# A quantised convolution and an involution on one core: each image's weights two stages earlier

## The chip, the cores and the metric

The kernel runs on one core of one Trainium2 chip. The metric is the device time of one execution in microseconds (us). The time before is the median of three runs, 1355.05 us (1355.0 to 1357.66). One further execution was profiled, and every row quoted from a profile is from it.

## What is computed

The input is a batch of 32 images with 256 channels of 32 x 32 pixels. Two layers follow each other, and each adds its result to its own input:

```
x = x + conv3x3_quantised(groupnorm(x)) + bias
x = x + involution(groupnorm(x))

involution(x):                       # 16 groups of 16 channels, 7 x 7 window
    y = relu(bn(w1 @ x))             # 256 -> 64 channels, per pixel
    w = w2 @ y + b2                  # 16 groups x 49 taps, per pixel
    out[g, c, pixel] = sum over 49 taps of w[g, tap, pixel] * x[g, c, neighbour(tap)]
```

The quantised convolution works on values rounded to ten mantissa bits, for which the kernel uses float16 operands. What is special about the involution is that its 7 x 7 weights differ from pixel to pixel: they must be computed for each image (784 of them per pixel) before the sums over neighbours can be made.

## The kernel before

**Engines and stages.** The program is written as one loop over stages (`for n in range(FRONT, B * per + 2)`, line 556), with `per = 16` stages to an image. Under `tc.manual_schedule()` each engine executes its instructions in the order in which the program issues them, so the order of the calls inside a stage is the order on every queue. `due(n, lag)` (line 549) turns a stage into an image `b` and a position `i` in 0..15: a step with lag -18 belongs to the image whose sums begin 18 stages later. Several images are therefore in work at once.

What an image `b` goes through, with stages counted from the start of its own sums (stage 0):

- Stage -63 (`LOAD`): its input `x` is loaded by SP, two DMAs (line 106). The tile pool has five image buffers, so this load waits for the output of image `b - 5`.
- Stages -56 to -7 (`FRONT`, the generator `front`): first group norm on ACT (lines 214 to 273), the 3 x 3 convolution on TensorE (line 332, nine matmuls in each odd stage), its clamp and residual add on DVE (lines 346, 348), second group norm, and at stage -20 the features: eight matmuls `py` (line 377), then two ACT activations that write `y_sb[b % 2]` (line 388). After that the normalised pixels are transposed by TensorE (`pt`, line 396) and copied by ACT into `pixels` (line 400).
- Stages -18, -16, ..., -4 (`LEAD = 18`, `weights`): eight blocks of 32 small matmuls `pw` (line 411), each for four image rows, that multiply `w2` with `y`. DVE adds the bias and writes the result into `w_sb` (line 435), a ring of 32 rows, that is one image. An inner block has four such evictions; the first and the last block of an image have eight smaller ones, because the window leaves the image there.
- `scatter` (line 465): when the rows of a quarter `k` (eight image rows) are complete, SP writes them from `w_sb` to `wd`, a DRAM buffer that holds one image. A quarter has seven DMAs of 160 KB (line 476): the four even ones one stage after the block that completes the quarter (blocks 2, 4, 6 and 7), the three odd ones one stage later. With the lag of 18 the four quarters start at stages -13, -9, -5 and -3. A quarter's rows in `wd` may be overwritten only once the previous image's band load of this quarter has read them.
- `load_bands` (line 478) at stages -9, -5, -1 and 3: a quarter's weights come back from `wd` in a skewed order into one of three `band` buffers, 16 DMAs (line 497), two issued by SP (`BY_SYNC`) and fourteen by POOL. The first needs all seven writes of its quarter and the buffer free from the sums three quarters before.
- Stages 0, 2, ..., 14: `sums`, 64 matmuls on band and pixels (line 522), two stages' worth to a quarter; one stage later DVE adds the result into `x` (line 538).
- Stages 12 and 15: `store` sends the two halves of the result out by SP (line 543).

**The order inside a stage** is: the fronts of all images in work, oldest first; `sums`; `add_windows` and `store`; `weights`; `scatter`; `load_x`; `load_bands`. So on TensorE a stage with features has `py`, then 64 sums matmuls of the image two before, then a block of weights matmuls of whichever image is due. Before the change the block in the stage of image `b`'s features is the last block of image `b - 1`.

**Queues.** SP issues input loads, weight writes, two sixteenths of the bands and the outputs, in order. POOL issues nearly nothing but its band transfers. Each of the two queues has eight semaphores for its DMAs in turn, so a DMA also waits for the one eight before it on its own queue.

Of the kernel before, what the change touches and what calls it, by code (L numbers as in the profile page):

```python
# [71 lines left out]
LATE = K1 * SW + 2 * 2 * SW  # L72
FRONT = -56
LOAD = -63
LEAD = 18


@with_exitstack
def tile_quant_conv_then_involution(
# [460 lines left out]
    def store(b, k):  # L540

        cols = slice(k * NT, (k + 1) * NT)
        nc.sync.dma_start(out[b].rearrange("(h p) n -> p h n", p=P)[:, :, cols], x_tiles[b][:, :, cols])
# [5 lines left out]
    def due(n, lag):  # L549

        b, i = divmod(n - lag, per)
        return (b, i) if 0 <= b < B else (None, None)

    with tc.manual_schedule():
        fronts = {}
        for n in range(FRONT, B * per + 2):
# [24 lines left out]
            if b is not None and i == 2 * (M - 1 - SIDES):  # L581
                store(b, 0)
            b, i = due(n, -LEAD)
            if b is not None and i % 2 == 0:
                weights(b, i // 2 * WR)

            for part in range(2):
                b, i = due(n, -LEAD + 1 + part)
                if b is not None and i % 2 == 0:
# [48 lines left out]
```

## Time and profile before

| | |
|---|---|
| median of the runs | 1355.05 us (1355.0 to 1357.66) |
| the profiled execution | 1344.24 us |
| its span, from the first to the last instruction | 1342.5 us |
| mean granted TensorE clock | 0.982 |
| data moved by DMA | 361.85 MB, mean 270 GB/s |
| weight writes, `wd<-w_sb` | 896 DMAs of 160 KB |
| band transfers issued by POOL / by SP | 1792 / 256 |
| one POOL band transfer: issue / from issue to landing | 549 ns / 4.6 us median |
| DVE waiting for weights matmuls | 419.2 us |
| POOL waiting for its own earlier band transfers | 182.0 us |
| POOL waiting for weight writes | 63.2 us, 37.1 of them once, at the start |
| PE waiting for bands | 42.7 us |
| SP waiting for outputs before it may load the next input | 77.1 us |

The table's waits are from the view that lists who waited for whom. An engine's wait costs time only if the engine is on the path that sets the end. DVE waits a lot here since it has the least to do. In the lists of groups, a row reads: line, engine, operation, what is written and read, shapes, count, then busy time and mean duration of one in ns, then the idle time before such instructions and what ended it. In the table of stretches an engine's figure is its busy time in that stretch, followed by the number of instructions; the last three columns are the granted TensorE clock, the mean busy share of the 16 DMA engines by packet time (overlapping packets can take it a little over 1), and GB/s.

### The profile page before, as it was taken

How to read it: one execution, taken by the hardware profiler on the slowest of the kernel's cores; microseconds unless marked ns; L12 is line 12 of the kernel's file. 1: busy time of each engine (PE TensorE's matmuls, PEld its weight loads, DVE VectorE, ACT ScalarE, POOL GpSimd, SP SyncE). 2: the span in 40 equal slices, each digit the busy share in tenths (PEclk: the TensorE clock that was granted, in tenths of full speed). 3: DMA queues.
4: the chain of work that ended last, by engine and by line, in shares of the span. 5: the costliest groups of instructions: out<-in, count | busy, mean ns of one | idle time of the engine just before them, and what ended most of it. 6: DMA issues, size and time to landing. Idle time of an engine off the chain costs nothing.

```text
span 1342.5 us, 65799 instructions
## 1 busy us (share of the span) xinstructions
PE 1253.6 (93%) x27648; PEld 763.7 (57%) x27648; DVE 818.8 (61%) x2539; ACT 733.3 (55%) x1731; POOL 1014.4 (76%) x1818
## 2 busy tenths in 40 slices
PE   5899999999999999999999999999999999999665
PEld 2356566565555655556655556666555566556454
DVE  3466666565666665656665666766666666666442
ACT  5775656455656556556545655655556564553300
POOL 9067878777787778777778787788777877788785
PEclk9999999999999999999999999999999999999987
DMA  6089999999999999999999999999999999999995
GB/s 228 11 237 295 271 293 293 279 266 281 272 286 282 291 285 270 283 263 280 293 282 283 270 288 282 293 297 296 281 288 275 277 284 290 271 281 266 278 274 166
DMA packets 360724, 361.85 MB, mean 270 GB/s; under 512 B 75056, under 2 KB 304752, under 8 KB 359152
## 3 DMA queue, kind: packets, MB, share of 16 engines
q1 hardware_dynamic: 278512, 229.38, 56.8%
q0 software_dynamic: 81920, 128.28, 33.9%
q8 instruction: 220, 3.60, 1.1%
q14 instruction: 72, 0.59, 0.1%
HBM read 176.60 MB, written 180.76 MB: 266 GB/s over the span
## 4 chain that ended last, share of the span: by engine, by line
PE 60%; DMA 23%; POOL 7%; issue 3%; ACT 3%; DVE 2%; SPq 1%; POOLq 0%; DVEq 0%; ACTq 0%
PE pc L332 25%; PE acc L522 19%; DMA band<-wd 17%; PE pw L411 11%; POOL band L497 7%; DMA wd<-w_sb 6%; PE pt L396 3%; PE py L377 3%; ACT junk L214 1%; SPq L476 1%; DVE w_sb L435 1%; DMA x<-in_x 1%; ACT xn L273 0%; SPq L497 0%; ACT xq L273 0%
## 5 line engine op out<-in xcount | busy, mean ns | idle before, releaser
L497 POOL DMA_DIRECT2D band<-wd x1792 | 980.3, 549 | 315.7 <-DMA band<-wd 182.0
L435 DVE TENSOR_TENSOR w_sb<-pw,late_sb 128x224 f32<-128x224 f32 (+7 forms) x1280 | 330.4, 322 | 419.5 <-PE pw L411 419.2
L332 PE MATMUL pc<-xq,wq 128*128 128x496 f16 (+3 forms) x2304 | 535.2, 379 | 20.3 <-ACT xq L273 18.3
L522 PE MATMUL acc<-band,pixels 64*32 64x190 f32 (+1 forms) x16384 | 426.6, 332 | 51.8 <-DMA band<-wd 42.7
L522 PEld LDWEIGHTS acc<-band,pixels 64*32 64x32 f32 x16384 | 304.7, 107 | 159.7 <-issue 81.1
L332 PEld LDWEIGHTS <-wq 128*128 128x128 f16 x2304 | 206.7, 98 | 316.1 <-issue 102.7
L411 PE MATMUL pw<-late_sb,y 64*32 64x224 f32 (+1 forms) x8192 | 288.9, 333 | 10.8 <-issue 9.4
L538 DVE TENSOR_TENSOR x<-acc,x 128x380 f32<-128x380 f32 (+1 forms) x512 | 262.0, 512 | 32.2 <-PE acc L522 23.2
L411 PEld LDWEIGHTS pw<-late_sb,y 64*32 64x32 f32 x8192 | 186.5, 106 | 38.1 <-issue 21.0
L400 ACT COPY pixels<-pt 128x512 f32<-128x512 f32 x128 | 73.7, 576 | 228.6 <-PE pt L396 228.6
L214 ACT ACTIVATE junk<-x 128x512 f16<-128x512 f32 (+1 forms) x192 | 146.4, 763 | 14.7 <-DVE x L348 12.2
L214 ACT ACTIVATE junk<-x,mean 128x1024 f16<-128x1024 f32 x128 | 147.1, 1149 | 4.3
L245 ACT ACTIVATE s<-back,eps 128x2 f32<-128x2 f32 x64 | 18.9, 296 | 178.6 <-DVE back L230 178.6
L346 DVE TENSOR_SCALAR q<-pc 128x512 f16<-128x512 f32 x128 | 87.2, 681 | 17.6 <-PE pc L332 17.6
L273 ACT ACTIVATE xn<-x,off,rstd 128x512 f32<-128x512 f32 x128 | 96.2, 800 | 0.0
L348 DVE SCALAR_TENSOR_TENSOR x<-q,early_sb,x 128x512 f32<-128x512 f16 x128 | 94.2, 736 | 0.3
L396 PEld LDWEIGHTS pt<-ident,xn 128*128 128x128 f32 x512 | 63.9, 142 | 26.3 <-issue 2.5
L396 PE MATMUL pt<-ident,xn 128*128 128x128 f32 x512 | 78.0, 275 | 0.1
L273 ACT ACTIVATE xq<-x,off,rstd 128x1024 f16<-128x1024 f32 x64 | 75.7, 1227 | 0.0
L235 ACT ACTIVATE mean<-back 128x2 f32<-128x2 f32 x64 | 12.6, 196 | 101.4 <-DVE back L230 101.4
L377 PE MATMUL py<-xn,early_sb 128*64 128x512 f32 x256 | 62.2, 606 | 0.9 <-ACT xn L273 0.9
L224 DVE STREAM_TRANSPOSE across<-sums 128x32 f32<-128x32 f32 x128 | 26.3, 205 | 33.6 <-ACT junk L214 32.4
(40 smaller groups left out, 369.3 us busy)
## 6 DMA issues: line engine op xcount, KB each, us to landing
wd<-w_sb SPq DMA_DIRECT2D x896, 160.0 KB
band<-wd POOLq DMA_DIRECT2D x1664, 70.5 KB, 4.6
x<-in_x SPq DMA_DIRECT2D x64, 512.0 KB
out<-x SPq DMA_DIRECT2D x64, 512.0 KB
band<-wd POOLq DMA_DIRECT2D x128, 60.5 KB, 4.6
band<-wd SPq DMA_DIRECT2D x128, 50.5 KB
band<-wd SPq DMA_DIRECT2D x128, 40.5 KB
band<-in_w SPq DMA_DIRECT2D x2, 1152.0 KB
```

What stands on the lines that cost most here:

```text
L214: nc.scalar.activation(junk[:, n0:n1], src[:, h, n0:n1], func, bias=bias, accum_out=self.sums[:, i : i + 1])
L273: nc.scalar.activation(dst, src, AF.Identity, bias=self.off[:, one], scale=self.rstd[:, one])
L332: nc.tensor.matmul(pc.rearrange("p (r c) -> p r c", c=W)[:, r0 - nt * RT : r1 - nt * RT, c0:c1], wq[:, kh, k, mh * P : (mh + 1) * P], xq[: ...
L346: nc.vector.tensor_scalar(q, pc, F16_MAX, -F16_MAX, ALU.min, ALU.max)
L348: nc.vector.scalar_tensor_tensor(xt[:, mh, cols], q, bias_sb[:, mh : mh + 1], xt[:, mh, cols], ALU.add, ALU.add)
L377: nc.tensor.matmul(py[i * CR : (i + 1) * CR], w1_sb[:, kh, :], px[:, :, i], start=kh == 0, stop=kh == CH - 1,)
L396: nc.tensor.transpose(pt[:, i, h * P : (h + 1) * P], xn[:, h, (m + i) * P : (m + i + 1) * P], ident)
L411: nc.tensor.matmul(pws[i][t * TW : (t + 1) * TW, : dj.stop - dj.start, r], y_sb[b % 2][half, (r0 // 2 + r) * W : (r0 // 2 + r + 1) * W], w ...
L435: nc.vector.tensor_tensor(to, of[:, :, d0:d1], bias[:, :, d0:d1], ALU.add)
L497: queue.dma_start(to, src)
L522: nc.tensor.matmul(at[t * TW : (t + 1) * TW, h, :, f - top : l - top], px[p, a, v * GC : v * GC + TW], of[:, :, a, f - top : l - top, v], ...
L538: nc.vector.tensor_tensor(x_at, of, x_at, ALU.add)
```

## The change

One constant changes:

```
-LEAD = 18
+LEAD = 20
```

`LEAD` is used in three places: `weights` (line 583) and both parts of `scatter` (line 588). All eight blocks of weights matmuls of an image, the evictions that follow them and the 28 writes to `wd` are issued two stages earlier with respect to that image's features, sums and band loads. The numbers of instructions stay as they are.

- The blocks now stand at stages -20, -18, ..., -6. The first one is issued in the stage of the image's own features: on TensorE `py`, the sums of another image, then the weights matmuls that read the `y` which ACT computes from `py`.
- The writes of the four quarters start at stages -15, -11, -7 and -5; the band loads stay at -9, -5, -1 and 3. Between a quarter's last write in program order and its band load there are now five stages instead of three (seven instead of five in the fourth quarter).
- A quarter's writes stand ten stages (eight in the fourth quarter) behind the previous image's band load of that quarter, instead of twelve (ten).
- On SP's queue, the four even writes of a first quarter now stand ahead of the input load of a later image, and its three odd writes right behind it; all seven stood behind that load. The even writes of a fourth quarter now stand ahead of the two SP band pieces of the second quarter, and its odd writes behind the first output; the whole quarter stood after that output.

## The prediction

> **What bounds the kernel now.** I read the page's first, third and fifth parts, then stretches of equal length, then the waits of POOL over the steady middle, then the chain of waits around one load, and last the rows of single instructions. The sum is made against the profiled execution: span 1342.5 us, 1344.24 us with what lies around it, which is 10.8 us under the median of the runs, 1355.05 us. I work out a difference and apply it to the median.
>
> ```profile
> span 1342.5 us, 65799 instructions
> PE 1253.6 (93%) x27648; PEld 763.7 (57%) x27648; DVE 818.8 (61%) x2539; ACT 733.3 (55%) x1731; POOL 1014.4 (76%) x1818
> ...
> DMA  6089999999999999999999999999999999999995
> ...
> q1 hardware_dynamic: 278512, 229.38, 56.8%
> q0 software_dynamic: 81920, 128.28, 33.9%
> ...
> L497 POOL DMA_DIRECT2D band<-wd x1792 | 980.3, 549 | 315.7 <-DMA band<-wd 182.0
> ...
> L522 PE MATMUL acc<-band,pixels 64*32 64x190 f32 (+1 forms) x16384 | 426.6, 332 | 51.8 <-DMA band<-wd 42.7
> ```
>
> Three things are nearly full at once: PE (93%), the DMA engines (56.8% for SP's transfers and 33.9% for POOL's) and POOL. POOL's busy 76% understates it. In the rows of its 1,792 band transfers, 14 to a load, 128 loads, the next load nearly always starts where the last ended, from 71.7 us to 1330.6 us; in between stand 980 us of issuing and the rest waiting. PE in its turn waits 42.7 us for bands.
>
> ```profile
> core 0: us, PE busy (x) PEld busy (x) DVE busy (x) ACT busy (x) POOL busy (x), PEclk, DMA share, GB/s
> ...
> 881.00:919.00 38.00, 38.00 (x866) 23.27 (x865) 25.32 (x80) 22.83 (x55) 31.34 (x58) 1.00 0.98 293
> 919.00:957.00 38.00, 38.00 (x865) 23.15 (x863) 25.25 (x79) 22.67 (x54) 29.33 (x54) 1.00 0.98 289
> 564.00:605.00 41.00, 38.35 (x857) 23.52 (x840) 24.16 (x77) 21.91 (x53) 30.14 (x56) 0.96 0.93 265
> ```
>
> Each of these is one image. In the first two PE never stops: 38.0 us is its floor. The third takes 41 us. By the first sums of images 0 and 29 (87.7 and 1236.1 us) the mean is 39.6 us, so 1.6 us an image is what no PE work explains.
>
> ```profile
> POOL band L497 <- DMA band<-wd: 168.0, 213, 2.9
> POOL band L497 <- issue: 50.7, 66, 3.2
> POOL band L497 <- DMA wd<-w_sb: 22.5, 24, 3.1
> ```
>
> These are POOL's waits from 103.4 to 1220.6 us. Only the third line is a wait for the weights' writes, which the change moves. The first is POOL waiting for its own transfers of eight before.
>
> ```profile
> 632.41 1.26 DVE w_sb L435 x4
> 633.67 0.47 DVE x L538
> ...
> 635.21 4.00 DMA wd<-w_sb
> ...
> 639.24 0.55 POOL band L497
> 639.79 4.86 DMA band<-wd
> ```
>
> The chain runs from the eviction over a write to POOL, but this link is doubtful: the POOL transfer at 639.24 is the last of its load, whose writes had been issued by 624.9 and had let its first transfer go at 630.9. So the page's share of 6% for wd<-w_sb is too high a price, and I count waits by their place in the load.
>
> **The change, part by part.** Nothing is added or removed; the 32 blocks of `weights` matmuls, their evictions and the 28 writes per image on SP stand two stages (of 16 per image, so 39.6/8 = 4.95 us) earlier against features, sums and band loads.
>
> POOL, the gain. Loads 4 to 115 are 28 of each quarter. A first transfer waits for the writes 12.8 us in all at the first quarter, 0.4 at the second, 2.3 and 3.4 at the third and fourth. At three of the latter (1.6, 1.8, 1.6 us) the last write had been issued 14 us or more before, so I leave both quarters out and take 13.2 us. The earlier start covers it: the longest of these waits is 1.9 us against 4.95. At the first quarter not all of 4.95 arrives, because the three odd writes now stand behind the next x load, but the four even ones stand ahead of it; four issues at about 0.83 us (seven took 5.76 us) still leave 3.3 us. Bounds: 0 to all 22.5 us.
>
> What comes back. Issuing sooner raises the share that SP's transfers take while POOL issues. Inside a load POOL waits 0.84, 2.22, 1.79 and 2.80 us in the four quarters, while SP's transfers take 0.52, 0.62, 0.54 and 0.66 of the DMA engines: 11.9 us per unit of share by a line through the four. An image shorter by x raises the mean share, 0.58, by 0.58x/39.6, and four loads then wait 4 × 11.9 × 0.58/39.6 = 0.70x longer. So the gain is 13.2/1.70 = 7.8 us, and with 22.5 it would be 13.2; with no feedback at all 22.5, with a full one 0.
>
> Here a rule speaks against the change. The row: during POOL's waits for writes the DMA engines were 1.02 busy by packet time, over 90 to 1240 us 0.965. The Trainium skill, "DMA: Bandwidth & Descriptors", section "Issuing engines are not separate DMA queues", says that transfers started by SP and POOL run on the same 16 engines and interleave; then an earlier write only makes a band transfer wait in its stead. By the rule the sum is 0 and the time 1355; by the row's 3.5% of free time something is left.
>
> PE, the loss. An image's first weights now stand in the stage of its features, behind 64 sums matmuls only, and need both y activations. y ends 1.07 to 1.40 us after the last py matmul, and the block that stands there now starts 1.17 to 1.25 us after it; its start would be held until 0.05 us after y, as it was at image 0. Over images 2 to 31 that is 3.3 us. At images 0 and 1 no sums stand between and y ends 3.0 us after py: PE idles 3.1 us each instead of 1.05 and 0.16, 4.9 us more. Behind the waiting matmuls stands the next convolution, and no band load waits for that. All 8.2 us are costed at nothing because PE waits 42.7 us for bands anyway; without that cover they cost 8.2 us.
>
> DVE and ACT. The two edge blocks take 1.89 us of evictions instead of 1.52 and move from stages 12 and 14 to 10 and 12; the narrowest margin of the sums' banks is 2.55 us, so nothing. ACT's order around y is the same.
>
> SP. A fourth quarter's writes overwrite what the previous image's fourth band load reads. That load's end plus the median 4.6 us to landing lies on average 0.5 us behind the eviction two stages earlier, behind it in 17 of 27 images, at most by 2.9 us, 16.9 us in all. Behind it on SP stand the odd writes, two band pieces, the first output and, four stages on, an x load. SP's band pieces are issued well before POOL's end; x lands 3.3 to 10.6 us before its first use. So nothing again; with that cover gone, the longest would cost 2.9 us an image. In exchange the four even writes of a first quarter stand ahead of the x load, where SP waits 77.1 us for outputs (2.9 us an image).
>
> The start: image 0's features end at 52.6 us and its weights start 3.07 us later in either order, so the first load moves by nothing. The end: the last loads are POOL's pace too, and gain nothing of their own.
>
> Sum: −7.8 us, 1355 − 8 = 1347 us; by the bounds 1332 to 1355.
>
> **The rivals.** "PE sets the pace": with the writes out of the way and SP not idle behind the x load, POOL gets ahead and all images take PE's 38.0 us. 29 × 1.6 = 46 us, less 10.8 us that PE loses before its own weights matmuls and 8.2 us at y: −27, 1328 us. For it: four images in a row (805 to 957 us) ran so, and buffers were free some 9 us before POOL used them. Against: in those four POOL's lead over PE shrank from 8.9 to 5.1 us, so POOL was the slower there too.
>
> "Nothing, since the wait changes its name": POOL waits for its own transfers just as long; 1355 us. For it: 1.02 busy in these waits. Against: 0.965 over all.
>
> "The writes now meet the first quarter's loads" (slower): first-quarter loads are the quick ones because SP's share is low there (0.52). With the writes two stages earlier these loads meet the third and fourth quarters' writes without a pause. If their inner wait rises from 0.84 to the mean of the four, 1.91, that is 1.07 × 31 = 33 us, less the 13.2: +20, 1375 us; if half of it comes back from the other quarters, +3, 1358. I take the middle, 1366. It decides from 13.2/31 = 0.42 us more per first-quarter load. For it: POOL has no slack, and the bunching is real: the pause between fourth- and first-quarter writes, which x and an output fill now, keeps only the output. Against: SP's total is unchanged, so other loads should gain what these lose.
>
> **How the numbers follow.** Forecast 0.37, PE's pace 0.13, nothing 0.15, slower 0.35. A measurement of this kernel can't tell less than about 0.2% (2.7 us) from no change. Faster is the first two, 0.50; same 0.15; slower 0.35. The likeliest time is the forecast's 1347 us, its own range 1332 to 1355. The range for 8 in 10 must hold both signs: from 1330, which leaves out the larger half of "PE's pace", to 1370, which leaves out a third of "slower".
>
> **What would show it.** The wait of POOL for wd<-w_sb should fall from 22.5 us over the same loads to under 5, and POOL's wait for its own transfers rise by 3 to 8 us from 168. If the first falls and the second rises by as much, it is "nothing"; by over 15 us more, and most of it in first-quarter loads, "slower". If images of 38.0 us become the rule and PE's wait for bands before the last three images falls below 10 us, it is "PE's pace". PE's wait for y should be about 9 us, 6 of them before 100 us; if it is over 20, my price of y was wrong. SP should show a new wait of some 15 us of fourth-quarter writes for band<-wd. The prediction is wrong if the first-quarter loads still wait for their writes, or if x lands late and ACT waits for it.

## The result and the profile after

The change makes the kernel slower. Its median over 12 runs is 1366.83 us (1362.56 to 1371.55), that of the kernel before, over 12 runs in turn with it, 1355.03 us (1347.15 to 1362.26). The ratio is 1.009, with a 95% interval from 1.0064 to 1.0116; the medians differ by 11.8 us. The profiled execution of the changed kernel took 1371.3 us and that of the kernel before 1344.24 us. The first is among the longest of its 12, the second shorter than all 12, so some 15 of the 27 us between the two spans are chance. What follows is read from places in the traces, not from the difference of the spans.

From the page of the changed kernel, its busy times and its groups of instructions:

```profile
span 1369.5 us, 65800 instructions
...
PE 1259.5 (92%) x27648; PEld 759.3 (55%) x27648; DVE 819.5 (60%) x2539; ACT 733.8 (54%) x1731; POOL 1014.6 (74%) x1818
...
L497 POOL DMA_DIRECT2D band<-wd x1792 | 980.5, 549 | 341.6 <-DMA band<-wd 215.0
...
L522 PE MATMUL acc<-band,pixels 64*32 64x190 f32 (+1 forms) x16384 | 429.4, 331 | 52.5 <-DMA band<-wd 25.6
...
L411 PE MATMUL pw<-late_sb,y 64*32 64x224 f32 (+1 forms) x8192 | 288.5, 330 | 27.5 <-issue 21.3
```

The work is the same: POOL still issues for 980 us. Its waits rose from 315.7 to 341.6 us. PE stands idle before the sums for as long as before (52.5 us against 51.8), but a smaller part of that is for bands (25.6 against 42.7). Before the weights matmuls it now stands 27.5 us, where it stood 10.8.

POOL's waits in the same stretch as shown for the kernel before, 103.4 to 1220.6 us (in all, times, longest):

```profile
POOL band L497 <- DMA band<-wd: 195.2, 251, 3.0
POOL band L497 <- issue: 42.0, 65, 2.5
POOL band L497 <- DMA wd<-w_sb: 13.6, 21, 1.8
POOL band L497 <- DMA x<-in_x: 7.6, 8, 1.8
```

The wait for the writes fell from 22.5 to 13.6 us, as the change suggests. The wait for POOL's own transfers rose from 168.0 to 195.2 us, three times as much, and 7.6 us of waits are put down to the input load, after 0.6.

Two images of the changed kernel, and then PE's waits from 140 to 1220 us, first of the changed kernel, then of the kernel before:

```profile
core 0: us, PE busy (x) PEld busy (x) DVE busy (x) ACT busy (x) POOL busy (x), PEclk, DMA share, GB/s
698.70:737.00 38.30, 38.30 (x865) 23.24 (x864) 25.27 (x80) 22.28 (x55) 29.34 (x54) 1.00 0.98 285
817.50:859.20 41.70, 39.21 (x871) 23.52 (x875) 24.39 (x78) 21.78 (x54) 33.52 (x62) 1.00 0.95 272
```

```profile
PE pw L411 <- issue: 17.5, 18, 1.8
PE acc L522 <- issue: 12.1, 11, 2.3
PE acc L522 <- DMA wd<-w_sb: 7.7, 8, 1.9
...
PE acc L522 <- DMA band<-wd: 0.9, 1, 0.9
```

```profile
PE acc L522 <- DMA band<-wd: 15.3, 13, 2.7
PE pw L411 <- issue: 8.2, 13, 1.1
PE acc L522 <- issue: 3.6, 5, 1.2
```

Some images still run without a stop, others take over 41 us. From the first sums of image 1 to those of image 29 an image takes 40.16 us on average, against 39.66 before. PE waits less for late bands (about 9 us, the lines of `wd<-w_sb` and `band<-wd` together, against 15 to 18) and far longer for nothing that the profile names: 31 us by "issue" against 12. One such stop on PE's timeline, in the midst of the 64 matmuls of a sum:

```profile
1033.65 0.56 PE L522 MATMUL acc<-band,pixels 64*32 64x190 f32 x15
1036.22 1.37 PE L522 MATMUL acc<-band,pixels 64*32 64x190 f32 x49 [2.01 <-issue]
```

After 15 of 64 matmuls PE executes nothing for 2 us, and the profile names no wait. The profile has a DMA queue of its own for instructions, the page's "q8 instruction": 220 transfers of 16,384 bytes, about one for every 256 instructions of PE. Four of the stops and the transfer that ended before each, from the trace of the changed kernel, in us:

```
PE stops   PE goes on   instruction transfer, start to end   from its end to PE
 351.01      353.36          350.82 to 351.92                     1.44
 393.04      394.63          392.25 to 393.36                     1.27
 480.02      481.71          479.29 to 480.22                     1.49
 833.82      835.58          833.18 to 834.30                     1.28
```

From 140 to 1220 us, all 24 unnamed stops over 0.25 us of the changed kernel, and all 17 of the kernel before, ended 1.2 to 1.8 us after the end of such a transfer, though one comes only every 6 us or so. So I read them as PE waiting for its own instructions; no run tried this alone. They gather in the fourth sums of an image: 20.2 us there after the change, 8.4 before.

### The profile page after: what moved, and what is told of

The parts are those of the page before. It is cut to its first block, busy times and chain, and to the rows that moved or that the text cites. A ratio compares the mean times of both kernels' runs of the same rounds, so it can differ in the third digit from the quotient of the medians.

```text
span 1369.5 us, 65800 instructions
## 1 busy us (share of the span) xinstructions
PE 1259.5 (92%) x27648; PEld 759.3 (55%) x27648; DVE 819.5 (60%) x2539; ACT 733.8 (54%) x1731; POOL 1014.6 (74%) x1818
## 4 chain that ended last, share of the span: by engine, by line
PE 76%; DMA 10%; issue 4%; ACT 4%; POOL 3%; DVE 2%; SPq 1%; POOLq 0%; ACTq 0%
PE pc L332 31%; PE acc L522 24%; PE pw L411 14%; DMA wd<-w_sb 7%; PE py L377 4%; PE pt L396 3%; POOL band L497 3%; DMA band<-wd 3%; ACT junk L214 1%; DVE w_sb L435 1%; SPq L476 1%; DMA band<-in_w 1%; ACT xn L273 0%; ACT xq L273 0%; ACT rstd L266 0%
## 5 line engine op out<-in xcount | busy, mean ns | idle before, releaser
L497 POOL DMA_DIRECT2D band<-wd x1792 | 980.5, 549 | 341.6 <-DMA band<-wd 215.0
L522 PE MATMUL acc<-band,pixels 64*32 64x190 f32 (+1 forms) x16384 | 429.4, 331 | 52.5 <-DMA band<-wd 25.6
L522 PEld LDWEIGHTS acc<-band,pixels 64*32 64x32 f32 x16384 | 301.4, 107 | 166.7 <-issue 93.5
L411 PE MATMUL pw<-late_sb,y 64*32 64x224 f32 (+1 forms) x8192 | 288.5, 330 | 27.5 <-issue 21.3
L538 DVE TENSOR_TENSOR x<-acc,x 128x380 f32<-128x380 f32 (+1 forms) x512 | 262.6, 513 | 39.5 <-PE acc L522 30.7
L224 DVE STREAM_TRANSPOSE across<-sums 128x32 f32<-128x32 f32 x128 | 26.3, 206 | 30.5 <-ACT junk L214 29.4
```

Source lines behind the costliest of these rows:

```text
L411: nc.tensor.matmul(pws[i][t * TW : (t + 1) * TW, : dj.stop - dj.start, r], y_sb[b % 2][half, (r0 // 2 + r) * W : (r0 // 2 + r + 1) * W], w ...
L497: queue.dma_start(to, src)
L522: nc.tensor.matmul(at[t * TW : (t + 1) * TW, h, :, f - top : l - top], px[p, a, v * GC : v * GC + TW], of[:, :, a, f - top : l - top, v], ...
L538: nc.vector.tensor_tensor(x_at, of, x_at, ALU.add)
```

## The experiments

Each is compared with the kernel before, run beside it on the same chip, whose median was 1355.31 us for e1 to e4, 1348.26 for e5 to e8, 1345.22 for e9 to e12, 1346.23 for e13 to e16 and 1345.41 for e17 and e18. "POOL" below is the time from the start of POOL's load 4 to the end of its load 115 in the one profile of each: 1108.8 us before, 1126.4 us after the change. "Stops" are PE's stops from 140 to 1220 us, the unnamed ones (by my reading, for instructions) + the others, mostly for late bands: 12.4 + 17.8 before, 31.3 + 9.2 after. Both are from one execution, and executions of one kernel differ by about 1% (1347.15 to 1362.26 us before the change), so the ratios decide and not these two.

**Is it the start, or the features' `y`?** Three edits of the changed kernel: the features one stage earlier (e1), image 3's input ahead of image 0's first writes (e2), and both (e3).

```
e1, e3:  in front(), before py:   stages(2) -> stages(1)
         in front(), after y:     stages(5) -> stages(6)
e2, e3:  ahead of the scatter loop:
+            if due(n, LOAD) == (3, 0):
+                x_tiles[3] = load_x(3)
```

> The kernel after, with the features (py and the two y activations) one stage earlier, so that a convolution half stands between py and the first weights again. Theory START (the +12 us are paid once, before the first sums: PE idles 3.1 us twice for y, runs at half clock after each, and reaches image 0's first sums 8.1 us later in the profiles): PE's wait for y falls from 6.2 to about 1 us, no half clock before the first sums, first sums at about 88 us instead of 95.8 if the bands are there; POOL's first load still starts at 76.6, so part stays: 1360 to 1363. Theory STEADY (the writes now collide with the band loads and SP's order is worse, some 0.4 us in each image): 1365 to 1368.

> The kernel after, with image 3's input load issued ahead of image 0's first writes, where it stood before the change, instead of between the even and the odd ones. START: POOL's first load starts at about 72 us instead of 76.6, since 1 MB no longer stands among the first writes; PE is late by y all the same, so 1362 to 1366. STEADY: no change, 1365 to 1368.

> The kernel after, with both: features one stage earlier, image 3's load ahead of the first writes. START: the first sums and the first load are where they were before, and the time is that of before or a little under it, 1348 to 1357. STEADY: 1364 to 1368. In between by the share of each.

Measured: e1 1364.9 us, 1.0064 [1.0037, 1.0091]; e2 1367.21 us, 1.0091 [1.0057, 1.0124]; e3 1362.39 us, 1.0061 [1.0032, 1.009]. In e2 POOL's first load starts at 71.0 us, where it started before the change (71.7, after it 76.6), and yet POOL takes 1126.3 us: the start is not the cause. `y` is at most a small part of it: e1's interval overlaps the change's.

**The weights early, the writes where they were.**

```
+WRITE = 18
-                b, i = due(n, -LEAD + 1 + part)
+                b, i = due(n, -WRITE + 1 + part)
```

> Weights and evictions two stages earlier as in the change, but the writes to DRAM left at their old stages. START by y alone: PE is late as in the change, POOL's first load starts near 72 us: 1360 to 1364. STEADY: the writes are where they were, so 1354 to 1358. If it is slower than the change, the early writes were a help and the early weights the harm.

Measured: 1354.56 us, 0.9993 [0.9966, 1.0019]; POOL 1109.8 us, stops 15.5 + 9.5. The whole loss goes with the writes. PE's order is that of the change, its first sums start at 96.4 us instead of 87.7, and nothing is lost by it: PE's waits for late bands fall by 8.3 us, about what the start is late.

**Which writes, and past what.** e5 writes only the first quarter early, e6 only the other three. e7 is the whole change with the input load moved ahead of the writes of its stage, so that all seven stand behind it again; e8 is the change with the input load two stages later, behind all seven.

```
e5, e6:  b, i = due(n, 1 + part - (LEAD if k == 0 else WRITE))     # e6: k > 0
e7:      the three lines of load_x moved ahead of "for part in range(2)"
e8:     -LOAD = -63
        +LOAD = -61
```

> Weights at the new place; only the first quarter's writes two stages earlier too, the other three quarters' writes at their old stages. Theory SPLIT (the harm is that a later image's input load, 1 MB, now stands between the even and the odd writes of the first quarter, so that writes wait for it: SP's wait of writes for x rose from 15 to 53 us): slow as the change, 1361 to 1367, and SP's wait of writes for x over 40 us. Theory PAUSE (the harm is that the writes of quarters two to four run ahead of the sums' stages, so that SP waits for evictions and outputs, the DMA engines stand at 0.73 in the ninth stage and over 1.05 in the fifth to seventh): as before, 1353 to 1358.

> Weights at the new place; the writes of quarters two to four two stages earlier, the first quarter's at its old place behind the input load. SPLIT: as before, 1353 to 1358. PAUSE: slow as the change, 1361 to 1367, with the ninth stage's DMA share under 0.85.

> The change, with each input load ahead of all seven first-quarter writes of its stage, as it stood before the change. SPLIT: most of the harm goes, 1354 to 1360. PAUSE: 1363 to 1369, and SP again waits some 75 us for outputs before it may load.

> The change, with each input load two stages later, behind all seven first-quarter writes. SPLIT: most of the harm goes, 1354 to 1360. PAUSE: 1363 to 1369. A third way: x lands too late for its group norm (its margin was 5 us and more), ACT waits for it, and the time is over 1370.

| | median us | ratio [95%] | POOL | stops |
|---|---|---|---|---|
| e5, first quarter early | 1356.98 | 1.0077 [1.005, 1.0105] | 1116.4 | 29.2 + 5.3 |
| e6, the others early | 1345.78 | 0.9988 [0.9957, 1.0019] | 1111.8 | 22.9 + 9.9 |
| e7, load ahead of all writes | 1349.14 | 1.0001 [0.9975, 1.0026] | 1107.1 | 19.3 + 4.9 |
| e8, load behind all writes | 1368.78 | 1.016 [1.0135, 1.0185] | 1128.9 | 26.3 + 12.0 |

The harm is in the first quarter's writes alone, and only where they stand ahead of an input load. My theory SPLIT, that the writes are harmed by an input load in their midst, fits e5, e6 and e7 and fails at e8: there nothing is split, and it is the slowest of all. PAUSE as I had put it, with the harm in quarters two to four, fails at e6. Nor is it the third way: in e8 ACT never waits for `x` from 140 to 1220 us.

In these four kernels the time goes with POOL's wait for its own transfers, from 140 to 1220 us: the kernel before, the changed one, e7 and e8.

```profile
POOL band L497 <- DMA band<-wd: 162.5, 207, 2.9
```

```profile
POOL band L497 <- DMA band<-wd: 188.8, 244, 3.0
```

```profile
POOL band L497 <- DMA band<-wd: 159.3, 204, 3.7
```

```profile
POOL band L497 <- DMA band<-wd: 200.4, 221, 3.9
```

SP's queue around the load of one image, in the kernel before, in the changed one and in e7 (start, duration, instructions):

```profile
1082.24 2.53 SPq L497 DMA_DIRECT2D band<-wd  x2
1086.97 0.84 SPq L106 DMA_DIRECT2D x<-in_x  x2
1088.16 2.81 SPq L476 DMA_DIRECT2D wd<-w_sb  x4
```

```profile
1101.14 2.29 SPq L497 DMA_DIRECT2D band<-wd  x2
1103.78 3.54 SPq L476 DMA_DIRECT2D wd<-w_sb  x4
1107.43 0.92 SPq L106 DMA_DIRECT2D x<-in_x  x2
1108.45 2.50 SPq L476 DMA_DIRECT2D wd<-w_sb  x3
```

```profile
1084.38 1.67 SPq L497 DMA_DIRECT2D band<-wd  x2
1089.00 1.29 SPq L106 DMA_DIRECT2D x<-in_x  x2
1090.65 3.54 SPq L476 DMA_DIRECT2D wd<-w_sb  x4
```

Before the change, and in e7, nothing is issued for 2.2 and 2.95 us ahead of the load: SP waits for the output that frees the buffer, and the writes stand behind that wait. In the changed kernel the four even writes go out into that pause and the other three follow the load at once. SP's waits over the whole execution say the same, here of the kernel before, the changed one and e7:

```profile
SPq L106 <- DMA out<-x: 77.1, 27, 4.1
```

```profile
SPq L476 <- DMA x<-in_x: 53.3, 38, 3.1
```

```profile
SPq L106 <- DMA out<-x: 75.4, 27, 4.4
```

The wait for outputs, 2.9 us an image, is all but gone from the changed kernel (1.5 us in all); instead its writes wait 53.3 us behind the input load (before: 17.3). The other runs go the same way: from 140 to 1220 us SP waits 81.0 us for outputs in e4 and 75.3 in e6, which lose nothing, but 3.4 in e5 and not at all in e8. So I read the wait, which looked like idle time, as what paced the writes.

The traces exclude a plainer cause, that the input load simply leaves too late. About when SP issues an input load, POOL starts the band load of the fourth quarter of an earlier image. On the mean of images 8 to 28, in the one profile of each, SP issues the input load 4.3 us ahead of that start in the kernel before and 4.2 us in e8, 8.1 us in the changed kernel and 8.2 us in e7: of each pair one is slow and the other isn't. The last of the four even writes is issued 0.9, 1.5, 5.3 and 5.0 us ahead of it in the kernel before, e4, e6 and e7, but 9.0, 8.6 and 7.9 us ahead in the changed kernel, e5 and e8.

**Is it the meeting with the input load?** e9 is the changed kernel and e10 the kernel before without the input loads of images 5 to 31: `load_x` returns the kept tile of image `b % 5`, so these images are computed from tiles that hold earlier results. e11 and e12 (kernel before; e4) were meant to spread the traffic instead: the second half of every input is loaded two stages after the first.

```
e9, e10:      if b >= 5:
                  return kept[b % 5]
e11, e12:     x_tiles[b] = load_x(b, range(1))
              b, i = due(n, LOAD + 2)
              if i == 0 and b is not None and b > 1:
                  nc.sync.dma_start(x_tiles[b][:, 1], x[b, P : 2 * P])
```

> The change without the input loads of images 5 to 31, whose buffers keep what they held (that part of the work is left out, and the values are not the reference's). Theory CROWD (the harm needs the input load: with the even first-quarter writes ahead of it, its 1 MB meets the odd writes, the third and fourth quarters' band loads and TensorE's instruction transfers in stages 5 to 8, the instruction transfers come late and PE stands still at the fourth sums): without the load no such stall is left; PE's stops of unnamed cause at the fourth sums fall from 20 us to under 6, and the time is within 4 us of the next run's, both well under 1355. Rival WRITES (the early writes harm by themselves): 8 to 12 us slower than the next run.

> The kernel before without the same input loads, for the comparison with the run above. CROWD: within 4 us of it. WRITES: 8 to 12 us faster than it.

> The kernel before, with the second half of each input loaded two stages after the first. A search for a better version by CROWD: 0.5 MB at a time, PE's unnamed stops at the fourth sums (8 us before) shrink, 1347 to 1354 where before has 1355; but if the second half lands just later in the same crowd, 1355 to 1362.

> Weights at their new place, writes at their old stages (the kernel of the fourth experiment, even with before), and the input in two halves two stages apart. CROWD: 1345 to 1353; otherwise even with before, or slower by as much as the second half is late.

Measured: e9 1312.9 us, 0.9758 [0.9722, 0.9795]; e10 1300.94 us, 0.9678 [0.9644, 0.9712]; e11 1351.97 us, 1.0049 [1.0021, 1.0076]; e12 1348.63 us, 1.0027 [1.0001, 1.0054]. e11 and e12 are slower, not faster (e12 only just clear of noise), and their edit does more than spread the load. The stage two after the load is that of the four even first-quarter writes, so the second half now stands behind them, as the whole load does in the changed kernel. SP's queue in e11:

```profile
1095.21 0.36 SPq L106 DMA_DIRECT2D x<-in_x  x1
1095.92 2.58 SPq L476 DMA_DIRECT2D wd<-w_sb  x4
1098.55 1.03 SPq L598 DMA_DIRECT2D x<-in_x  x1
```

With half the bytes behind writes that are not early, they lose 0.5 and 0.3%, although SP keeps its wait for outputs (78.5 us in e11). That fits the order in the queue as the cause; it shows that some loss comes with the pause kept, too.

Without the load the change still costs 12 us, and my expectation that the two would then lie within 4 us failed. But it isn't the same loss: the stops are nearly gone (3.9 + 0 us in e9, 5.3 + 1.4 in e10). POOL's waits from 140 to 1220 us, of e9 and then of e10, show another regime:

```profile
POOL band L501 <- DMA band<-wd: 101.9, 142, 2.0
POOL band L501 <- PE acc L526: 59.0, 55, 2.9
```

```profile
POOL band L501 <- DMA band<-wd: 114.7, 160, 2.7
POOL band L501 <- issue: 45.3, 61, 2.9
```

In e9 POOL waits 59 us for PE to free band buffers, which it did for 0.2 us in the changed kernel with its loads. PE sets the pace there, busy for 1076 of these 1080 us (1072 in e10), so that PE's own losses count: first sums at 96.5 us instead of 87.6, and 1072.3 us from image 1 to image 29 instead of 1065.1. The latter is `y`: from 140 to 1220 us PE's weight loads wait 6.9 us for it in e9, and never in e10.

**PE's losses uncovered, three attempts.** e13 is e9 with the features one stage earlier. e17 is e4, so the change's order on PE with the writes back, and e18 is the kernel before with the features two stages later (`stages(2)` to `stages(4)`, `stages(5)` to `stages(3)`); all three without the input loads of images 5 to 31.

> The change without the input loads of images 5 to 31 (left out as in the ninth run), and with the features one stage earlier. Theory COVER (without the loads PE sets the pace; the 12 us that stay between the ninth and the tenth run are y: first sums 9 us later, then a held start in most images): even with the tenth run, ratio to before 0.965 to 0.971, first sums near 88 us. Rival WRITES (the early writes harm by themselves, whatever the input load): it stays 8 to 12 us slower than the tenth run, ratio 0.974 to 0.979.

> Weights two stages earlier, writes to DRAM where they were, and the input loads of images 5 to 31 left out (those images are computed from the inputs kept of images 0 to 4). The question is what made the change 12 us slower than the kernel before when neither loads these inputs. Cover (PE's late start and its held y, 8.9 + 7.2 us, count there because nothing else stops PE): this kernel has the same PE order as the change, so it should lose the same: ratio to the kernel before 0.973 to 0.979, first sums at 96 us, as the change without inputs (0.976). Writes (the earlier writes cost time even without input loads): with the writes back it should stand at 0.966 to 0.970, even with the kernel before without inputs (0.968).

> The kernel before without the input loads of images 5 to 31, and only the features' matmuls py moved two stages later, so that the first weights of an image stand right behind its own features as in the change, while weights, writes and loads stay. Cover: held y costs 5 to 9 us over images 1 to 29 where PE sets the pace, and the start moves by 0 to 9 us: ratio to the kernel before 0.972 to 0.979. Writes: the PE order is not the cause, ratio 0.966 to 0.970.

Measured: e13 1315.17 us, 0.9757 [0.9724, 0.9791]; e17 1312.95 us, 0.9753 [0.9722, 0.9783]; e18 1306.39 us, 0.9712 [0.9678, 0.9747]. e13 tells nothing: PE waited for the normalised pixels ahead of the features instead (first sums at 93.9 us). e17 decides: the same order on PE with the writes put back loses what e9 loses, and PE's weight loads wait 7.3 us for `y`, so without the loads the loss is PE's, not the writes'. In e18 the features alone cost about 5 us against e10, by the two ratios; its ratio lies just below the span that I gave for "cover", and its interval reaches into both.

**Is there a better kernel in it?** e7, e6 and e4, each with the features one stage earlier as in e1.

> The change with the input loads ahead of the first-quarter writes (the seventh run, even with before) and the features one stage earlier. COVER and CROWD: nothing of the crowd is left and y costs nothing, so at most what y still cost there: ratio 0.992 to 1.000. WRITES: no better than the seventh run, 1.000 or more.

> First-quarter writes at their old place, the other three quarters' two stages earlier (the sixth run, 0.9988 of before), and the features one stage earlier. COVER: 0.990 to 0.999. If y is covered by waits for bands there too: 0.998 to 1.002.

> Weights two stages earlier, all writes at their old stages (the fourth run, 0.9993 of before), and the features one stage earlier. COVER: the fourth run was even with before although PE reached its first sums 9 us later, so y was covered there and this gives 0.994 to 1.001.

Measured: e14 1345.53 us, 0.9988 [0.9959, 1.0016]; e15 1347.96 us, 0.9995 [0.9967, 1.0023]; e16 1345.72 us, 0.999 [0.9965, 1.0015]. None can be told from the kernel before. `y` early gains nothing where its cost is covered.

## Why the prediction was wrong

It said 1347 us, by a gain of 7.8; it was 1366.83, a loss of 11.8. By its own steps:

- **POOL's gain, 13.2 us at the first quarter.** Right in kind, two thirds in size: by the rows of the first transfers that wait fell from 12.8 to 4.1 us, so 8.7 us were gained. Why the rest stayed isn't shown: in e1 and e2, with the same order on SP, 0.6 and 0.5 us are left.
- **"What comes back", 5.4 us. The step that failed.** POOL's wait for its own transfers rose by 27.2 us. I had worked the return out from the mean share of SP's transfers and the image's length, as if it didn't matter in which order SP's queue issues them. It does: with the writes as early in the program and only the load put ahead of them (e7) this wait is 159.3 us from 140 to 1220 us, against 188.8 in the changed kernel and 162.5 before. Inside a load POOL waited 0.84, 2.22, 1.79 and 2.80 us in the four quarters; now it is 1.16, 1.90, 2.65 and 2.64, and in e8 the fourth stands out (4.13). No single quarter is the mark of the loss, though: the third is at 2.55 and 2.52 in e6 and e7 too, which lose nothing.
- **SP, "In exchange the four even writes of a first quarter stand ahead of the x load, where SP waits 77.1 us for outputs".** Booked at nothing, without a reason, and the place of the harm: e5 makes only the first quarter's writes earlier and is slower by 0.8%, e7 puts only the load ahead of them again and is even with the kernel before.
- **PE, 8.2 us at `y`, costed at nothing.** Right, and shown by e4: late by 8.7 us at the first sums, at no loss. "Without that cover they cost 8.2 us" was right in kind too: e9 and e17 have no such cover and lose 12 and, by the ratios, about 10 us. The size was short: at the start I counted PE's two idles, 4.9 us, and not the slow matmuls after them (below; 8.8 us late in e9), and afterwards 3.3 us, where e9 took 7.2 us more from image 1 to image 29. PE's wait for `y` before 100 us was 6.2 us, as forecast.
- **The start, "so the first load moves by nothing".** Wrong: image 3's input was queued behind image 0's first writes and was issued at 66.3 us instead of 14.8, and POOL's first load moved from 71.7 to 76.6 us. In e2 it is put right and nothing comes of it.
- **SP's wait of fourth-quarter writes for the band's reads,** 15 us forecast, 7.2 us measured from 140 to 1220 us; nothing was behind it, as forecast.
- **The rivals.** "Slower" gave 1366 us and so the right time, but by luck, since by its own mark it isn't what happened: a first-quarter load waits 0.32 us more, under the 0.42 from which it decides, and over 28 loads that makes 9 of the 27 us. "Nothing" had the right idea, that the wait changes its name; e6 shows just that, with 8 us less waiting for writes and 12 us more for POOL's own transfers (each from 140 to 1220 us), and no change of the kernel's time. "PE sets the pace" is wrong with the input loads and right without them (38.0 us an image in e10).

The rule I weighed, from the Trainium skill, "DMA: Bandwidth & Descriptors", section "Issuing engines are not separate DMA queues", that transfers interleave on the same engines whoever starts them, agrees with e10: fewer transfers on SP's queue, and POOL's wait for its own fell from 162.5 to 114.7 us (140 to 1220 us). It would have made the sum 0, nearer than my row's 3.5% of free time did; the loss itself comes from the order in the queue.

**What stays open.** That the loss comes from first-quarter writes that stand ahead of an input load on SP's queue is shown by e5 and e7: where the whole load stands ahead of all seven (before, e4, e6, e7) nothing is lost; where four of them stand ahead of it (the change, e5) the loss is 0.8 to 0.9%; where all seven do (e8), 1.6%. By what way this order costs time isn't shown. That the writes, no longer held up by SP's wait for outputs, meet other transfers in a crowd is my reading; e9 and e10 agree with it in that the stops go with the input loads. Nor does the loss always stand in the same wait: in e5 POOL's wait for its own transfers is only 169.8 us from 140 to 1220 us, while the first transfers of its fourth-quarter loads wait 15.2 us for writes (3.4 before). And the runs did not separate POOL's longer waits from PE's unnamed stops. In the changed kernel POOL waits for PE's sums 0.2 us in all, and the buffers stand free 6.9 us on average before it uses them; PE's stops fill time in which it would otherwise have waited for bands. In e8, the slowest, they are fewer (26.3 us) than in the changed kernel (31.3). I take POOL's transfers for what sets the long-run pace, but no run cured one symptom and left the other.

## What to carry to other kernels

Where the transfer engines are full, the order of transfers in an in-order DMA queue can cost time though their number stays: before moving work past a wait in such a queue, ask what would then leave in that pause and what it would meet. Price such a move by the order in the queue stage by stage; a mean share of the engines can't see it. Test a shift of several steps by undoing each queue crossing alone: here one of them held the whole loss. And ask of each new edit whether it makes such a crossing itself, as the halved loads did here.

## What the hardware showed that was not expected

**Instructions come by DMA too.** The page lists their queue, 220 transfers of 16 KB, with a share of 1.1% of the 16 DMA engines. PE's stops of up to 2.4 us that no wait explains ended 1.2 to 1.8 us after such a transfer, before and after the change; from 140 to 1220 us they took 12 us of PE's time before, 31 us after, and 4 to 5 us where the input loads were left out (e9, e10). Whether such a transfer is held up behind the others, and by what rule, wasn't tried.

**A short idle costs twice.** PE's idle ahead of the first weights, from its timeline, and the granted clock (third column from the end) in the idle and after it:

```profile
54.54 1.62 PE L411 MATMUL pw<-late_sb,y 64*32 64x224 f32 x32 [3.08 <-ACT y L388]
56.09 3.07 PE L332 MATMUL pc<-xq,wq 128*128 128x512 f16 x9
...
60.00 2.08 PE L332 MATMUL pc<-xq,wq 128*128 128x496 f16 x9
```

```profile
51.46:54.54 3.08, 0.00 (x2) 0.00 (x1) 0.00 (x0) 2.99 (x6) 0.00 (x0) 1.00 0.00 0
54.54:58.10 3.56, 3.56 (x37) 1.49 (x38) 1.72 (x9) 0.00 (x0) 0.00 (x0) 0.53 0.01 2
58.10:62.00 3.90, 3.90 (x46) 1.62 (x44) 2.34 (x9) 2.75 (x12) 0.00 (x0) 0.99 0.00 0
```

After 3.08 us without a matmul the clock is at half for 3.4 us, and nine convolution matmuls take 3.07 us instead of 2.08. The same happens at 85.2 us. An idle of 2.71 us some 33 us into the span was followed by a slow stretch in the kernel before (0.60 from 36.2 to 39.6 us) and not in the changed one (1.00 from 36.1 to 39.5 us). The Trainium skill, "TensorE: Matmul & The Clock Gate", section "HAM oscillation — how this bites in real kernels", gives over about 3.4 us of idle as the limit; by these rows a gap of 3.08 us is enough, and one of 2.7 us can be.
